# A selective scan with the decays of every third tile made in two column halves

## The chip, the cores and the metric

The kernel runs on one core of a Trainium2 chip. The metric is the device time of one execution in microseconds (us); less is better. The engines of the core are TensorE (PE in the profile, its weight loads PEld), VectorE (DVE), ScalarE (ACT), GpSimd (POOL) and SyncE (SP), which issues the DMAs. Each takes its instructions in the order in which they were written and waits on semaphores for the others.

## The reference

Two layers are computed on `x` of shape 8 x 64 x 64 x 96, in float32. The second, an MLP at doubled resolution with low-pass filters on both sides, fills time between the steps of the first. The first is a two-dimensional selective scan (SS2D); its core, cut to what matters, is this:

```python
# K = 4 directions, D_INNER = 192 channels, D_STATE = 16 states, L = 64*64 steps
def step(h, inp):
    ul, dl, Bl, Cl = inp
    dA = jnp.exp(dl[..., None] * A)                              # the decays
    h = dA * h + (dl * ul)[..., None] * Bl[:, :, None, :]        # the scan
    y = jnp.einsum('bkdn,bkn->bkd', h, Cl)                       # sum over the states
    return (h, y)
...
x = x + L0(group_norm(x))   # projection, 3x3 convolution, scans, layer norm, gate, projection
x = x + L1(group_norm(x))   # upsample, W1, quadratic, W2, low-pass, downsample
```

## The kernel before

An image, a direction and a chunk of `T` = 1024 steps have 192 x 16 state rows. They are cut into `NT` = 24 tiles of 128 partitions (8 channels x 16 states) and 1024 columns (steps). Eight images, four directions and four chunks make 3072 tiles. `t["i"]` is the number of a tile within its chunk, 0 to 23.

What a tile goes through, with the lines of the profile:

- `fetch` (L1063): a DMA brings `dub`, delta times input, spread over the 16 states.
- `product_b` (L1069): GpSimd multiplies it by `br` into `bb`, the scan's additive term.
- `decay` (L1075, L1082): TensorE spreads delta (`dl`) over the 16 states with a selection matrix `sel_b`. Two matmuls of 64 rows, one for each half of the columns, each fill one 2 KB bank of the tile `pd` (128 x 1024 float32 in PSUM, two banks). Float32 matmuls run as two passes, so the profile shows four. Then ScalarE takes the exponential of `pd` in place, scaled by `neg_a`, one number for each partition.
- `scan` (L1089): VectorE runs the recurrence over the 1024 columns. Its result overwrites `pd`, or, where the tile is a "GpSimd tile", goes into `h` in SBUF.
- `product_c` (L1095): the result times `cr` gives `hc`. Every third tile (`by_pool`, where `i % 3 == 2`) has this on GpSimd, from `h`; the others have it on VectorE, from `pd`.
- `hold` (L1108): the last column is copied to `carry` for the next chunk, by ScalarE in a GpSimd tile, by VectorE in the others.
- `sums` (L1127, L1139): TensorE sums `hc` over the states into `py`, for two tiles at a time; `store` copies it out (L1160).

`pd` has two buffers (`psd`, `bufs=2`), so the decay of a tile can begin once the tile two before it has released its buffer. In a GpSimd tile the scan itself releases it; otherwise the product and the copy of the carry do.

The order is written out by hand, in one loop over the tiles. In turn `i` these are issued: `fetch` six tiles ahead, the GpSimd product of the tile before, `product_b` three tiles ahead, `decay` of the next tile, then `scan`, `product_c` and `hold` of this one:

```python
if 0 < i <= n and tiles[i - 1]["by_pool"]:
    product_c(tiles[i - 1])
if i + LEAD < n:
    product_b(tiles[i + LEAD])
if i + 1 < n:
    decay(tiles[i + 1])
if t:
    scan(t)
    if not t["by_pool"]:
        product_c(t)
    hold(t)
```

After that `side.advance` hands out pieces of the other work (projections and the preparation of the next chunk, the convolution, layer norm, the MLP's rows) within a budget for each engine and turn (`CAPS`), `turn_over` (L1101) puts in a filler matmul `idle` where the side work gave TensorE little, and the sums follow. The budgets know neither the scans nor the decays; their costs are in no plan.

So on VectorE a GpSimd tile's scan is followed at once by the next tile's scan, unless side work of VectorE lies between; the other scans are followed by a product and a copy. The framework derives the semaphores from which tiles the instructions touch.

Of the kernel before, what the change touches and what calls it, by code (L numbers as in the profile page):

```python
# [9 lines left out]
AF = mybir.ActivationFunctionType  # L10
# [14 lines left out]
MB = 512  # L25
# [111 lines left out]
def kernel(ctx: ExitStack, tc: tile.TileContext, a: dict, out: bass.AP):  # L137
    nc = tc.nc
# [53 lines left out]
    neg_a = cp.tile([128, K, NT], F32, name="neg_a")  # L192
# [10 lines left out]
    sel_b = cp.tile([128, 8, NS, 8], F32, name="sel_b")  # L203
# [838 lines left out]
    for b in range(images):  # L1042
        for k in (1, 0, 2, 3):
            order = range(NCH) if k < 2 else range(NCH - 1, -1, -1)
            for n, c in enumerate(order):
                got = {}
                for i in range(NT):
                    q, n8 = divmod(i, 8)
                    s, j = n8 % 2, n8 // 2
# [20 lines left out]

    def decay(t):
        pd = t["pd"] = psd.tile([128, T], F32, tag="pd", name="pd")
        for hf in range(2):
            rows = slice(64 * hf, 64 * hf + 64)
            nc.tensor.matmul(  # L1075
                pd[:, MB * hf : MB * hf + MB],
                sel_b[rows, 4 * t["s"] + t["j"]].rearrange("p n c -> p (n c)"),
                t["got"]["dl"][rows, t["q"], :],
                start=True,
                stop=True,  # L1080
            )
        nc.scalar.activation(pd, pd, AF.Exp, scale=neg_a[:, t["k"], t["g"] : t["g"] + 1])  # L1082

    def scan(t):
        step = 1 if t["k"] < 2 else -1
# [86 lines left out]
    with tc.manual_schedule():  # L1172
# [3 lines left out]
        start, rest = front(0)  # L1176
# [8 lines left out]
        n = len(tiles)  # L1185
        for i in range(FETCH):
            fetch(tiles[i])
            if i >= FETCH - LEAD:
                product_b(tiles[i - FETCH + LEAD])
        decay(tiles[0])  # L1190
        begin, *side.later = prepare(0, tiles[NT]["k"], tiles[NT]["i0"], tiles[NT]["got"])
        total = 1
        for i in range(n + 4):
            t = tiles[i] if i < n else None
            at = i % (NT * NCH * K)
            if t and t["i"] == 0:
                b = t["b"]
                if at == 0:
# [9 lines left out]
                    if b + 1 < images:  # L1208
                        start, rest = front(b + 1)
# [31 lines left out]
            if i + 1 < n:  # L1241
                decay(tiles[i + 1])
# [110 lines left out]
```

## Time and profile before

| | |
|---|---|
| time of three runs | 11110.65, 11111.8, 11118.07 us; median 11111.8 |
| profiled execution | span of 11105.8 us from first to last instruction, 6.0 us below the median run; its time outside the span is not in the page |
| granted TensorE clock | 0.982 |
| PE busy | 9967.9 us, of it 3512.7 in the decays' matmuls and 932.0 in the filler |
| DVE busy | 10207.5 us |
| ACT busy | 5910.6 us, of it 3340.7 in the decays' exponentials |
| POOL busy | 10179.6 us |
| scan, 128 x 1024 | 2.34 to 2.35 us (2.28 to 2.29 in a direction's first chunk) |
| product on VectorE, on GpSimd | 1.23 us, 2.36 us |
| exponential, 128 x 1024 | 1.09 us |

A row of the costliest groups reads: line, engine, operation, output and inputs, shapes, count, then busy us and mean ns of one, then idle time of the engine just before, and what ended most of it. A wait is put down to the event that came last by the profile. The slowest core is the only one.

### The profile page before, as it was taken

Reading aid. Unit: us, or ns where it says so; the run is one execution under the profiler, and the core shown is the slowest. Engines: PE = TensorE matmul, PEld = TensorE weight load, DVE = VectorE, ACT = ScalarE, POOL = GpSimd, SP = SyncE. Lnnn points to the kernel's source line nnn. Section 1 sums busy time; section 2 is a strip of 40 time slices with the busy share of each in tenths; the row PEclk is TensorE's granted clock in tenths of the full one; section 3 lists DMA queues with packets and bytes.
Section 4 is the critical chain, followed back from the end, with each engine's and each line's share of the span. In section 5 each row is a group of like instructions: output and inputs, shape, how many; then the busy total and the mean of one; then the engine's idle time right before and its main releaser. Section 6 shows DMA issues by size and latency. Waiting matters only on the chain. (4 is left out here: it accounts for less than half of the span.)

```text
span 11105.8 us, 137238 instructions
## 1 busy us (share of the span) xinstructions
PE 9967.9 (90%) x45020; PEld 3204.6 (29%) x45020; DVE 10207.5 (92%) x7702; ACT 5910.6 (53%) x8218; POOL 10179.6 (92%) x4674
## 2 busy tenths in 40 slices
PE   8898888989889998999889998899988989889988
PEld 2222222322233222332223322233222332223325
DVE  6999999999999999999999999999999999999990
ACT  5455445656455564555545555455554655545543
POOL 5999999999999999999999999999999999999990
PEclk9999999999999999999999999999999999999998
DMA  6888898898988989888988989889898898988981
GB/s 174 215 208 224 209 231 209 217 227 232 233 209 216 225 231 225 212 218 224 240 217 215 224 221 244 209 219 225 217 243 210 217 228 218 247 206 216 227 214 48
DMA packets 1044463, 2401.27 MB, mean 216 GB/s; under 512 B 293820, under 2 KB 314556, under 8 KB 1043752
## 3 DMA queue, kind: packets, MB, share of 16 engines
q1 hardware_dynamic: 1042776, 2391.45, 86.5%
q8 instruction: 361, 5.91, 0.2%
q14 instruction: 350, 2.87, 0.1%
q10 hardware_dynamic: 976, 1.04, 0.0%
HBM read 1929.05 MB, written 328.73 MB: 203 GB/s over the span
## 5 line engine op out<-in xcount | busy, mean ns | idle before, releaser
L1069 POOL TENSOR_TENSOR bb<-dub,br 128x1024 f32<-128x1024 f32 x3072 | 7173.5, 2359 | 208.4 <-DMA dub<-du 149.2
L1082 ACT ACTIVATE pd<-pd,neg_a 128x1024 f32<-128x1024 f32 x3072 | 3340.7, 1088 | 4533.0 <-PE pd L1075 4489.8
L1075 PE MATMUL pd<-dl,sel_b 64*128 64x512 f32 x12288 | 3512.7, 645 | 987.2 <-DVE carry L1108 649.2
L1089 DVE TENSOR_TENSOR_SCAN pd<-pd,carry,bb 128x1024 f32<-128x1024 f32 x1536 | 3610.3, 2350 | 262.2 <-ACT carry L1108 127.9
L1095 POOL TENSOR_TENSOR hc<-h,cr 128x1024 f32<-128x1024 f32 x1024 | 2413.9, 2357 | 352.6 <-DVE h L1089 300.7
L1095 DVE TENSOR_TENSOR hc<-pd,cr 128x1024 f32<-128x1024 f32 x2048 | 2508.4, 1225 | 164.1 <-PE py L1127 20.0
L1075 PEld LDWEIGHTS pd<-dl,sel_b 64*128 64x128 f32 x12288 | 966.7, 186 | 3266.3 <-issue 1511.2
L1089 DVE TENSOR_TENSOR_SCAN h<-pd,carry,bb 128x1024 f32<-128x1024 f32 x768 | 1797.3, 2340 | 5.8 <-ACT pd L1082 5.6
L1127 PE MATMUL py<-hc,sel_r 128*32 128x512 f32 x12288 | 1715.0, 617 | 30.4 <-POOL hc L1095 30.2
L1089 DVE TENSOR_TENSOR_SCAN pd<-pd,bb 128x1024 f32<-128x1024 f32 x512 | 1172.5, 2290 | 98.6 <-ACT carry L1108 75.3
L1101 PE MATMUL idle<-sel_b,ident 128*128 128x512 f32 x1652 | 932.0, 646 | 8.0 <-DVE ty L720 5.9
L562 PE MATMUL pc<-pad,convr 96*128 96x512 f32 (+1 forms) x2304 | 858.3, 616 | 5.7 <-DVE e L585 3.6
L1089 DVE TENSOR_TENSOR_SCAN h<-pd,bb 128x1024 f32<-128x1024 f32 x256 | 583.6, 2280 | 26.0 <-ACT pd L1082 25.2
L1127 PEld LDWEIGHTS py<-hc,sel_r 128*32 128x32 f32 x12288 | 250.3, 109 | 1109.0 <-issue 854.5
L1031 POOL TENSOR_TENSOR u<-dl,u 128x512 f32<-128x512 f32 x384 | 485.0, 1271 | 79.2 <-DVE dl L1028 79.2
L862 PEld LDWEIGHTS p<-w2q,mq 128*100 128x100 f32 x4800 | 452.9, 168 | 274.6 <-issue 214.2
L855 PE MATMUL ph<-xu,w 96*128 96x500 f32 x960 | 504.9, 629 | 11.5 <-ACT mq L856 6.7
L862 PE MATMUL p<-w2q,mq 128*100 128x96 f32 x4800 | 511.5, 258 | 2.3 <-ACT mq L856 2.3
L562 PEld LDWEIGHTS pc<-pad,convr 96*128 96x128 f32 (+1 forms) x2304 | 266.3, 163 | 563.9 <-issue 552.8
L987 PE MATMUL px<-u,xp 64*64 64x512 f32 x1536 | 422.4, 627 | 2.4 <-issue 2.4
L1101 PEld LDWEIGHTS idle<-sel_b,ident 128*128 128x128 f32 x1652 | 249.8, 189 | 596.5 <-issue 522.4
L1012 PE MATMUL pv<-xd,dt_w 64*64 64x512 f32 x1536 | 394.4, 609 | 1.0 <-ACT xd L997 1.0
(153 smaller groups left out, 6707.9 us busy)
## 6 DMA issues: line engine op xcount, KB each, us to landing
dub<-du SPq DMA_DIRECT2D x3072, 512.0 KB
u<-u SPq DMA_DIRECT2D x256, 384.0 KB
du<-u SPq DMA_DIRECT2D x768, 128.0 KB
y<-yq SPq DMA_DIRECT2D x768, 128.0 KB
br<-xd SPq DMA_DIRECT2D x256, 256.0 KB
cr<-xd SPq DMA_DIRECT2D x256, 256.0 KB
yp<-y SPq DMA_DIRECT2D x384, 128.0 KB
yp<-u SPq DMA_DIRECT2D x192, 128.0 KB
```

Source lines behind the costliest of these rows:

```text
L562: nc.tensor.matmul(t[rows].rearrange("p (i j) -> p i j", i=8), weights[:, cs], v["pad"][:, 8 * blk + kw : 8 * blk + kw + 8, kh : kh + H], ...
L855: nc.tensor.matmul(t[:, :px], w1[:, m, :], xu, start=True, stop=True)
L862: nc.tensor.matmul(t[:SIDE, C * i : C * i + C], sq[:, m, row], w2q[:, m, :], start=(m == 0), stop=(m == 2))
L987: nc.tensor.matmul(p[rows], xp[rows, k, q, :], v["u"][rows, q, :], start=(q == 0), stop=(q == 2), skip_group_check=True,)
L1031: nc.gpsimd.tensor_tensor(v["u"][:, q, :], got["dl"][:, q, :], v["u"][:, q, :], ALU.mult)
L1069: nc.gpsimd.tensor_tensor(t["bb"], t["dub"], t["got"]["br"], ALU.mult)
L1075: nc.tensor.matmul(pd[:, MB * hf : MB * hf + MB], sel_b[rows, 4 * t["s"] + t["j"]].rearrange("p n c -> p (n c)"), t["got"]["dl"][rows, t[" ...
L1082: nc.scalar.activation(pd, pd, AF.Exp, scale=neg_a[:, t["k"], t["g"] : t["g"] + 1])
L1089: nc.vector.tensor_tensor_scan(t["h"][:, ::step], pd[:, ::step], t["bb"][:, ::step], 0.0 if t["first"] else held, ALU.mult, ALU.add)
L1095: (nc.gpsimd if t["by_pool"] else nc.vector).tensor_tensor(t["hc"], t["h"], t["got"]["cr"], ALU.mult)
L1101: nc.tensor.matmul(p, ident, sel_b[:, 0:4].rearrange("p j n c -> p (j n c)"), start=True, stop=True)
L1127: nc.tensor.matmul(py[r0 : r0 + 32], sel_r[:, t["j"], :], t["hc"][:, MB * hf : MB * hf + MB], start=(t["j"] == 0), stop=(t["j"] == 3 and t ...
```

## The change

In `decay`, the tiles with `i % 3 == 0`, those that follow a GpSimd tile, are made in two column halves. The halves are cut within each bank: first columns 0 to 255 of both banks, by two matmuls of 256 columns, and their exponential as one instruction over 128 x 2 x 256; then columns 256 to 511 of both banks in the same way. The other tiles are as before. `skip_group_check` is a flag of the build and adds no instruction.

```diff
     def decay(t):
         pd = t["pd"] = psd.tile([128, T], F32, tag="pd", name="pd")
-        for hf in range(2):
-            rows = slice(64 * hf, 64 * hf + 64)
-            nc.tensor.matmul(
-                pd[:, MB * hf : MB * hf + MB],
-                sel_b[rows, 4 * t["s"] + t["j"]].rearrange("p n c -> p (n c)"),
-                t["got"]["dl"][rows, t["q"], :],
-                start=True,
-                stop=True,
-            )
-        nc.scalar.activation(pd, pd, AF.Exp, scale=neg_a[:, t["k"], t["g"] : t["g"] + 1])
+        parts = 2 if t["i"] % 3 == 0 else 1
+        w = MB // parts
+        scale = neg_a[:, t["k"], t["g"] : t["g"] + 1]
+        for c0 in range(0, MB, w):
+            for hf in range(2):
+                rows = slice(64 * hf, 64 * hf + 64)
+                nc.tensor.matmul(
+                    pd[:, MB * hf + c0 : MB * hf + c0 + w],
+                    sel_b[rows, 4 * t["s"] + t["j"]].rearrange("p n c -> p (n c)"),
+                    t["got"]["dl"][rows, t["q"], c0 : c0 + w],
+                    start=True,
+                    stop=True,
+                    skip_group_check=True,
+                )
+            part = pd.rearrange("p (a t) -> p a t", a=2)[:, :, c0 : c0 + w] if parts > 1 else pd
+            nc.scalar.activation(part, part, AF.Exp, scale=scale)
```

## Prediction

> **What bounds the kernel now.** First the page: busy shares, and PE in 40 slices.
>
> ```profile
> PE 9967.9 (90%) x45020; PEld 3204.6 (29%) x45020; DVE 10207.5 (92%) x7702; ACT 5910.6 (53%) x8218; POOL 10179.6 (92%) x4674
> PE   8898888989889998999889998899988989889988
> ```
>
> Three engines stand at 90 to 92%, so no share names the bound; it has to be read from waits. Next, the chain of waits on DVE, which runs all scans (waiting line, releaser, us in total, times, longest):
>
> ```profile
> DVE pd L1089 <- ACT carry L1108: 203.2, 414, 3.6
> DVE pd L1089 <- ACT pd L1082: 113.8, 238, 8.0
> DVE pd L1089 <- POOL bb L1069: 40.2, 38, 2.3
> ```
>
> The scans wait for ScalarE 652 times, 317.0 us in all, and hardly for GpSimd. The label "carry" is the last ACT event before the scan; the timeline shows what was really awaited (start, length, engine, line):
>
> ```profile
> 5014.67 0.15 DVE L1108 COPY carry<-pd 128x1 f32<-128x1 f32 x1
> 5014.74 2.34 DVE L1089 TENSOR_TENSOR_SCAN h<-pd,carry,bb 128x1024 f32<-128x1024 f32 x1
> ...
> 5014.97 1.13 PE L1075 MATMUL pd<-dl,sel_b 64*128 64x512 f32 x4 [1.31 <-DVE carry L1108]
> ...
> 5016.02 0.64 PE L914 MATMUL pn<-ident,x 128*96 128x128 f32 x4
> 5016.13 1.09 ACT L1082 ACTIVATE pd<-pd,neg_a 128x1024 f32<-128x1024 f32 x1 [2.77 <-PE pd L1075]
> ...
> 5017.32 2.36 DVE L1089 TENSOR_TENSOR_SCAN pd<-pd,carry,bb 128x1024 f32<-128x1024 f32 x1 [0.24 <-ACT carry L1108]
> ```
>
> The scan at 5014.74 is a GpSimd tile's (it writes h). Its successor is a tile of the change. The successor's `pd` comes free when DVE has copied the carry (5014.82); four profiled matmuls (two program matmuls, two passes each) end at 5016.10, the exponential at 5017.22, and 0.10 later the scan starts. DVE was done at 5017.08 and idled 0.24 us. After the other tiles DVE has a 1.23 us product and a copy to do, which cover the same chain; after a GpSimd tile it has not. Read tile by tile, in 622 of the 1024 changed tiles the scan starts within 0.15 us of its exponential's end; in the other 402 the median slack is 0.35 us. So DVE paces the kernel, and ahead of every third scan the chain matmul, exponential, scan sets DVE's pace.
>
> Last, one stretch of an image in windows of 100 us (busy us of each engine, instructions):
>
> ```profile
> 3277.00:3377.00 100.00, 95.76 (x541) 40.05 (x541) 96.43 (x74) 60.09 (x86) 97.22 (x44) 1.00 0.92 220
> 3377.00:3477.00 100.00, 97.60 (x540) 38.86 (x538) 96.00 (x59) 61.78 (x82) 97.03 (x45) 1.00 0.87 214
> 3477.00:3577.00 100.00, 96.49 (x543) 38.91 (x541) 96.07 (x76) 59.91 (x86) 98.63 (x46) 1.00 0.88 223
> ...
> 3777.00:3877.00 100.00, 98.95 (x398) 26.66 (x397) 95.31 (x75) 53.56 (x70) 94.98 (x43) 1.00 0.85 214
> 3877.00:3977.00 100.00, 95.78 (x392) 25.23 (x388) 95.44 (x76) 59.30 (x82) 93.30 (x43) 1.00 0.84 213
> ...
> 4077.00:4177.00 100.00, 85.45 (x324) 21.40 (x324) 95.98 (x72) 57.79 (x77) 89.81 (x41) 0.98 0.93 237
> ```
>
> First column: PE. In five of the fourteen windows from 2777 to 4177 PE is 96 to 99% busy: there it bounds beside DVE, with 4.24, 2.40, 3.51, 1.05 and 4.22 us left, 3.08 on average. In the other nine 8.8 to 16.2 us are left.
>
> **What the built order of the change shows.** DVE, GpSimd and the DMA queue keep their instructions and order. PE gets 2048 program matmuls more (4096 profiled), ACT 1024 exponentials. In every split tile the third matmul (second half, first row group) waits for ScalarE's semaphore at the count that the first half's exponential sets. Both halves write both banks of `pd` (columns 0 to 255 of each, then 256 to 511), and the exponential of a half spans both. So the halves do not overlap: matmul, exponential, matmul, exponential run one after the other.
>
> **The chain, step by step.** The costs of a half:
>
> ```profile
> L1082 ACT ACTIVATE pd<-pd,neg_a 128x1024 f32<-128x1024 f32 x3072 | 3340.7, 1088 | 4533.0 <-PE pd L1075 4489.8 <-DVE pd L1089 22.3 <-DVE h L1089 5.8
> L712 ACT ACTIVATE pn<-pn,eps 96x512 f32<-96x512 f32 x64 | 41.8, 653 | 26.0 <-PE pn L710 26.0
> ```
>
> Exponential of 512 columns: 0.65 us, by L712, in place in PSUM with one pointer operand; bounds 0.54 (half of 1.088) and 0.70 (L997, 696 ns). The Trainium skill, "ScalarE: Activation LUTs", What ACT_TABLE_LOAD costs, gives 280 ns plus 0.833 ns an element with one pointer operand: an estimate of 0.71 for a half, 1.13 for the whole that the trace has at 1.09; by it the two halves together grow against the whole by 0.08 more, and the total by some 60 us. Matmuls of a half: 0.64 us, by the four 128-column ones of L914 (512 columns one after another, as here two passes of 256, the row groups side by side); bounds 0.57 (half of 1.13) and 0.70 (0.06 for two exposed weight loads). PE to ACT takes 0.05 us or less here, ACT back to PE 0.05 (shortest pair, L997 to L1012).
>
> Now 1.13 + 0.05 + 1.09 = 2.27. Then 0.64 + 0.05 + 0.65 + 0.05 + 0.64 + 0.05 + 0.65 = 2.73. The chain grows by **0.46 us**; by the bounds by 0.10 to 0.68. In 622 tiles nothing covers it: 622 x 0.46 = 286 us. In the other 402 DVE's own side work covers part; what remains of 0.46 beyond each tile's slack sums to about 45. Together 331 us, over the 10716 us that the scans take 3.09 per 100 us.
>
> PE is held from the first matmul to the last for 0.64 + 0.05 + 0.65 + 0.05 + 0.64 = 2.03 instead of 1.13: **0.90 us** longer. Queued behind the waiting matmul are the sums into `py`, the side work's matmuls (convolutions, projections, MLP), the idle filler and the next decay. With 9.56 changed tiles per 100 us that is 8.60. In nine windows of fourteen PE's own gaps of 8.8 or more hide it; were they gone it would cost what the full windows pay. In the five full windows it does not fit: if the gaps shrink from 3.08 to 1.05, the fullest window's, 2.03 is swallowed and 6.57 is left. That covers the 3.09 of the scan chain there (the two lie side by side).
>
> Sum per 100 us: 5/14 x 6.57 + 9/14 x 3.09 = 2.35 + 1.99 = 4.33; times 107.2 gives **464 us**. The profiled span of 11105.8 becomes 11570. The median run, 11111.8, lies 6.0 above that span; with the same on top, **11576 us**.
>
> What costs nothing: ACT waits some 0.69 us between its halves, 710 us in all, with the carry copy, the copies out of `py` and side activations behind it; ACT sits idle 4533 us before exponentials today, and that is the cover. Gone, it would be 0.69 us in each tile. The next decay after a changed one comes 0.90 later on PE while DVE moves by 0.46; the 0.44 between lies under that tile's median slack of 0.72 (lower quartile 0.43), read tile by tile like those above; the quarter below it is part of what the full windows pay. Weight loads (4096 more) run beside matmuls but for the first, which the 0.64 holds.
>
> The trace of before never shows an exponential beginning before all matmuls of its tile have ended. The Trainium skill, "PSUM — Partial Sum Buffer", PSUM bank collisions raise a hardware error, says that two engines may not touch one bank in the same 32 partitions at once, even at disjoint columns, and that semaphores should guard by bank. By this rule the wait must be there, and the sum is the one above; were only the columns to count, it would be the first rival's.
>
> **Rivals.** *Not slower: the halves overlap.* If the first half's exponential were past when PE reaches the third matmul, ACT would run its first half beside the second matmuls: 0.64 + 0.05 + 0.65 + 0.65 = 1.99, 0.28 less than 2.27. Then waits such as the 0.24 at 5017.32 vanish: 622 x 0.24 = 149 us, 10963. It decides from the point where the third matmul comes less than 0.29 us after the second's end instead of 0.75 (0.64 + 0.29 + 0.64 + 0.05 + 0.65 = 2.27, as today). For it speaks only the change's shape; against it the semaphore count. 3%.
>
> *GpSimd or slack absorbs most.* GpSimd is at 95% in the full windows; if PE's lateness vanishes in its queues and the halves cost 0.60, only the scan chain counts, grown by 0.36: 622 x 0.36 + 23 = 247, to 331 at most: 11359 to 11443. For it: next tiles' slack. Against: scans wait for GpSimd 40 us in all. 22%.
>
> *PE becomes the bound.* If its gaps do not shrink in any stretch, since they are waits for DVE that only move, each tile pays 0.90: 1024 x 0.90 = 922, 12034. For it: PE at 96 to 99% in a third of the time. Against: 8.8 us and more free elsewhere. 8%. *Nothing measurable* (within 0.2%, some 22 us, about what a measurement here tells from no change): 3%.
>
> **Numbers.** The forecast has 64%: 11576, itself 11440 to 11710. The range, 11380 to 11790, reaches down to most of the absorbing case and up by the dearest half: 8.6 kept whole in the full windows (5/14 x 8.6 = 3.07) and the chain grown by 0.64 in the others (622 x 0.64 + 86 = 484 us, 4.52 per 100; 9/14 of it 2.90) give 5.97 per 100 us or 640 us, 11752, and the dearest half, 0.68, some 20 more; the end is set a little above for the PE-bound case. Faster 3%, same 3%, slower 94%.
>
> **What would show it.** Right: 256-column matmuls in two bursts with an exponential of about 0.65 between them; PE waiting about 0.7 us for ACT at the decay line, near 1000 times; scans after GpSimd tiles idle 0.7 us instead of 0.24; the windows full of PE work lengthened most. Wrong: an ACT half that starts before the last matmul of the other has ended (overlap); halves of 0.54; DVE's waits for ACT at 317 us or below; or the full windows growing no more than the light ones, which strikes the PE term.

## The result, and the profile after

The changed kernel takes 11880.73 us (median of 4 runs), the kernel before in the same session 11114.93: a ratio of 1.069 (95% interval 1.0676 to 1.0704), 766 us more. Slower, as forecast, but outside the range and 302 us beyond the 464 of the sum. The profiled execution has a span of 11882.6 us and a mean granted clock of 0.970 (0.982 before).

The page after, busy shares and PE in 40 slices:

```profile
PE 10337.2 (87%) x49116; PEld 3534.4 (30%) x49116; DVE 10260.5 (86%) x7702; ACT 6144.7 (52%) x9242; POOL 10204.4 (86%) x4674
...
PE   8888888988889888898888888888888989889888
```

The shares of PE, DVE, ACT and POOL all fell: none of the four became busier by as much as the span grew. The time went into waits. Line numbers shift from kernel to kernel: the decay's matmuls and exponential, L1075 and L1082 before, are L1079 and L1088 here, the scan, L1089 before, is L1095. The chain of waits, PE's and then DVE's (who waits, for whom, us, times, longest):

```profile
PE pd L1079 <- ACT pd L1088: 852.6, 1024, 6.6
PE pd L1079 <- DVE carry L1114: 394.3, 536, 2.6
PE pd L1079 <- DVE hc L1101: 186.6, 189, 3.3
```

```profile
DVE pd L1095 <- ACT pd L1088: 847.6, 784, 9.1
DVE pd L1095 <- issue: 141.6, 264, 1.5
...
DVE pd L1095 <- POOL bb L1069: 40.7, 53, 1.5
```

The first line is the wait that the built order showed: in all 1024 split tiles PE waits for an exponential, 0.83 us on average. DVE's waits for ScalarE ahead of scans whose result goes to `pd` rose from 317.0 us to 847.6, with a further 141.6 without a named releaser. One split tile and its successor on the timeline:

```profile
549.83 0.15 DVE L1114 COPY carry<-pd 128x1 f32<-128x1 f32 x1
549.90 2.28 DVE L1095 TENSOR_TENSOR_SCAN h<-pd,bb 128x1024 f32<-128x1024 f32 x1
...
550.13 0.70 PE L1079 MATMUL pd<-dl,sel_b 64*128 64x256 f32 x4 [1.47 <-DVE carry L1114]
550.87 0.66 ACT L1088 ACTIVATE pd<-pd,neg_a 128x512 f32<-128x512 f32 x1 [2.26 <-PE pd L1079]
...
551.59 0.70 PE L1079 MATMUL pd<-dl,sel_b 64*128 64x256 f32 x4 [0.75 <-ACT pd L1088]
...
552.22 2.07 PE L1107 MATMUL idle<-sel_b,ident 128*128 128x512 f32 x2
...
552.39 0.66 ACT L1088 ACTIVATE pd<-pd,neg_a 128x512 f32<-128x512 f32 x1 [0.86 <-PE pd L1079]
...
553.14 2.30 DVE L1095 TENSOR_TENSOR_SCAN pd<-pd,bb 128x1024 f32<-128x1024 f32 x1 [0.97 <-ACT pd L1088]
...
554.22 1.74 PE L1133 MATMUL py<-hc,sel_r 128*32 128x512 f32 x8
...
555.89 1.13 PE L1079 MATMUL pd<-dl,sel_b 64*128 64x512 f32 x4
...
557.07 1.09 ACT L1088 ACTIVATE pd<-pd,neg_a 128x1024 f32<-128x1024 f32 x1 [3.42 <-PE pd L1079]
...
557.15 0.15 DVE L1114 COPY carry<-pd 128x1 f32<-128x1 f32 x1
...
558.26 2.30 DVE L1095 TENSOR_TENSOR_SCAN pd<-pd,bb 128x1024 f32<-128x1024 f32 x1 [0.96 <-ACT pd L1088]
```

Three parts of the loss can be seen in it. *The chain:* from 550.13 to 553.05 it runs matmul, exponential, matmul, exponential, 2.92 us (median over the split tiles 2.94, against 2.27 before), and DVE idles 0.97 us. *The hold:* PE leaves the tile at 552.29 instead of 551.26, so filler, sums and the next decay (555.89) come late, and DVE idles 0.96 us once more ahead of the successor's scan at 558.26. *The clock:* the profile has a granted clock of 0.50 from 552.2 to 555.6; the filler takes 2.07 us and the eight matmuls into `py` 1.74, where they took 1.02 and 1.06 at the full clock. So in this example the clock has as much to do with the successor's 0.96 us as the hold has.

Read tile by tile, DVE's idle time ahead of the scans, by the place of the tile (us):

| kernel | tile after a GpSimd tile (split in the change) | the next | GpSimd tile |
|---|---|---|---|
| before | 311 | 36 | 32 |
| after | 828 | 200 | 35 |

517 of the 766 us lie ahead of the split tiles' own scans, 164 ahead of their successors'. (Summed over every gap of the trace, the first column is 9 to 21 us higher in all the kernels below; the differences hardly change.) Of the idle time ahead of the successors 133 us fall on the 132 tiles for which the clock stood at 0.50 somewhere between the split decay and the end of their own. That shows where the low clock is, not what it costs; e13 below measures that.

### The profile page after: what moved, and what is told of

It reads as the page before. It is cut to its first block, busy times and chain, and to the rows that moved or that the text cites. A ratio compares the mean times of both kernels' runs of the same rounds, so it can differ in the third digit from the quotient of the medians.

```text
span 11882.6 us, 147253 instructions
## 1 busy us (share of the span) xinstructions
PE 10337.2 (87%) x49116; PEld 3534.4 (30%) x49116; DVE 10260.5 (86%) x7702; ACT 6144.7 (52%) x9242; POOL 10204.4 (86%) x4674
## 3 DMA queue, kind: packets, MB, share of 16 engines
q10 hardware_dynamic: 976, 1.04, 0.0%
## 5 line engine op out<-in xcount | busy, mean ns | idle before, releaser
L1088 ACT ACTIVATE pd<-pd,neg_a 128x512 f32<-128x512 f32 (+1 forms) x4096 | 3580.9, 874 | 5075.4 <-PE pd L1079 4945.1
L1079 PE MATMUL pd<-dl,sel_b 64*128 64x256 f32 (+1 forms) x16384 | 3834.3, 542 | 1462.7 <-ACT pd L1088 852.6
L1095 DVE TENSOR_TENSOR_SCAN pd<-pd,carry,bb 128x1024 f32<-128x1024 f32 x1536 | 3614.0, 2353 | 757.2 <-ACT pd L1088 613.1
L1079 PEld LDWEIGHTS pd<-dl,sel_b 64*128 64x128 f32 x16384 | 1285.4, 188 | 4173.1 <-issue 1559.2
L1095 DVE TENSOR_TENSOR_SCAN h<-pd,carry,bb 128x1024 f32<-128x1024 f32 x768 | 1798.0, 2341 | 16.4 <-ACT pd L1088 12.5
L1095 DVE TENSOR_TENSOR_SCAN pd<-pd,bb 128x1024 f32<-128x1024 f32 x512 | 1174.6, 2294 | 291.3 <-ACT pd L1088 234.5
L1107 PE MATMUL idle<-sel_b,ident 128*128 128x512 f32 x1652 | 972.4, 672 | 0.4 <-DVE ty L720 0.4
L1095 DVE TENSOR_TENSOR_SCAN h<-pd,bb 128x1024 f32<-128x1024 f32 x256 | 584.1, 2282 | 19.3 <-ACT pd L1088 18.1
```

The lines of the kernel that those rows point to most:

```text
L1079: nc.tensor.matmul(pd[:, MB * hf + c0 : MB * hf + c0 + w], sel_b[rows, 4 * t["s"] + t["j"]].rearrange("p n c -> p (n c)"), t["got"]["dl"][ ...
L1088: nc.scalar.activation(part, part, AF.Exp, scale=scale)
L1095: nc.vector.tensor_tensor_scan(t["h"][:, ::step], pd[:, ::step], t["bb"][:, ::step], 0.0 if t["first"] else held, ALU.mult, ALU.add)
L1107: nc.tensor.matmul(p, ident, sel_b[:, 0:4].rearrange("p j n c -> p (j n c)"), start=True, stop=True)
```

## Experiments

Differences are against the kernel before in the same session (11110 to 11121 us).

**Split without the hold (e1).** The four matmuls first, then both exponentials: all the change's instructions, no matmul waiting for ScalarE.

```diff
-            part = ...
-            nc.scalar.activation(part, part, AF.Exp, scale=scale)
+        for c0 in range(0, MB, w):
+            part = ...
+            nc.scalar.activation(part, part, AF.Exp, scale=scale)
```

> Split as in the change, but all four matmuls of a split tile are issued before its two exponentials: the same number of instructions on every engine, and no matmul waits for an exponential. Theory A (the loss is the chain, longer by 0.67 us in the changed kernel's trace, plus PE held between the halves): the chain becomes about 1.33 + 0.05 + 0.66 + 0.05 + 0.66 = 2.75 us, 0.48 over the 2.27 of before; 622 x 0.48 + 47 = 346 us, PE held only some 0.2 us longer, in all 11400 to 11500. Rival R1 (the split work as such costs it, 4096 more matmuls and 1024 more exponentials, whatever waits for what): 11880 as in the changed kernel. Rival R2 (PE's hold alone costs it, DVE's chain is covered): 0.2 of 1.03 us of hold, some 150 us, 11265.

Measured: 11209.29, ratio 1.0084 (1.0068 to 1.0099), 89 us. So R1 falls: the split work as such does not cost 766 us. The same timeline rows in this kernel:

```profile
5011.24 1.14 PE L1079 MATMUL pd<-dl,sel_b 64*128 64x256 f32 x8 [1.47 <-DVE carry L1115]
...
5012.41 1.36 ACT L1089 ACTIVATE pd<-pd,neg_a 128x512 f32<-128x512 f32 x2 [2.53 <-PE pd L1079]
```

Back to back, eight half-width matmuls take 1.14 us, no longer than four whole ones (1.13); only apart do they cost 2 x 0.70. The two exponentials take 1.36 instead of 1.09. My 1.33 for the eight was wrong, and the chain grew by 0.26 us (median), not 0.48. The slack sum, each tile's growth less its slack, added up as in the prediction, makes 169 us of 0.26; the run pays about half of it.

**The matmuls alone (e2), the exponentials alone (e3).**

```diff
# e2: decay() of the change with one exponential after all four matmuls
-            part = ...; nc.scalar.activation(part, part, AF.Exp, scale=scale)
+        nc.scalar.activation(pd, pd, AF.Exp, scale=scale)
# e3: the kernel before, with
+        for part in (pd[:, :MB], pd[:, MB:]) if t["i"] % 3 == 0 else (pd,):
+            nc.scalar.activation(part, part, AF.Exp, scale=scale)
```

> Only the matmuls of every third tile are split, its exponential is one instruction again, after all four. A: chain 1.33 + 0.05 + 1.09 = 2.47, 0.20 over before: 622 x 0.20 and a little, 127 us, and as much as 40 for PE's 0.2 us: 11240 to 11280. R1: the matmuls' share of the 766 us, some half, 11500. R2: 11265 (does not part from A here).

Measured: 11119.55, ratio 0.9999 (0.9989 to 1.0008). Splitting the matmuls costs nothing where no wait lies between them; A's 127 us rested on the 1.33.

> Matmuls whole as before; in every third tile two exponentials of 512 columns, one for each bank. A: chain 1.13 + 0.05 + 0.66 + 0.06 + 0.66 = 2.56, 0.29 over before, PE not held: 199 us at 0.30, 11300 to 11320. R1: the exponentials' share of 766 us, 11500. R2: PE is not held, 11112 as before.

Measured: 11227.87, ratio 1.0097 (1.0082 to 1.0112), 108 us for a chain longer by 0.26. R2 (the hold is everything) falls, since nothing held PE here. But 0.26 by the slack sum would be some 170 us; the run pays 0.64 of it. Halves by bank did not overlap either: in none of the 1024 tiles does the first bank's exponential start before all four matmuls have ended, and the last passes of the two banks end 0.04 us apart.

**The split elsewhere (e4, e9).** A' in what follows is theory A as revised after e1 to e4: a longer chain costs less than its slack sum, and the hold comes on top, at the next decay behind it.

```diff
-        parts = 2 if t["i"] % 3 == 0 else 1
+        parts = 2 if t["i"] % 3 == 2 else 1     # e4; == 1 in e9
```

> The split as in the change, on the GpSimd tiles themselves (i % 3 == 2) instead of those after them: their chain has a median slack of 1.0 us, so a chain longer by 0.67 shows in few. But PE's hold of 1.03 us ends right ahead of the decay of the tile after, which has no slack in 622 cases. A: by the slack of each tile in the trace of before, 88 us for the chain and 485 for the hold beyond it: 11600 to 11700. Chain alone (no weight for the hold): 11200. R1: 11880.

Measured: 11843.33, ratio 1.0653 (1.0635 to 1.0671), 723 us, almost the change's loss, though the split tiles' own chains are covered. DVE's waits say whose scans are late:

```profile
DVE pd L1095 <- ACT carry L1114: 653.6, 563, 5.4
DVE pd L1095 <- ACT pd L1088: 318.0, 320, 8.0
DVE h L1095 <- ACT pd L1088: 93.7, 176, 6.1
```

The split tiles write `h` and wait 93.7 us. The scans into `pd` wait 971.6: the hold makes the decay of the next tile late, and here that is the one without slack (939 us of idle ahead of those scans, 311 before). The 573 us expected were too few, but the clock stands between: at 0.962 it is lower than the change's 0.970, and 93 of the decays without slack took over 1.3 us instead of 1.13 (22 before). How much of the 150 us beyond the expectation is the clock's, and how much the hold's, this run does not tell.

> The split on the tiles ahead of the GpSimd tiles (i % 3 == 1): their chain has a median slack of 0.72 us, and the decay after it, the GpSimd tile's, one of 1.0 us. A': by the slacks of the trace of before the longer chain (0.67) comes through with 161 us and the hold (1.03) beyond it with 113: 11390, the cheapest of the three places. Rival R1 (the split work as such): 11880 here too, as in both other places.

Measured: 11568.86, ratio 1.0409 (1.0395 to 1.0423), 458 us at a clock of 0.988. The cheapest place, as expected, but dearer than 274: the idle time is 170, 147 and 450 us ahead of split tile, successor and the one after, so tiles up to two decays on are late.

**Chain without hold, hold without chain, both.** e5 makes the exponential in four pieces (chain +0.79 us by its median), e14 in four or three in turn (+0.66 on average); e6 adds a filler matmul behind the decay, e15 does both.

```diff
# e14 (e5: all four cuts whenever i % 3 == 0)
+        cuts = (0, T) if t["i"] % 3 else (0, 256, 512, 768, T) if t["i"] % 6 else (0, 256, 512, T)
+        for c0, c1 in zip(cuts, cuts[1:]):
+            nc.scalar.activation(pd[:, c0:c1], pd[:, c0:c1], AF.Exp, scale=scale)
# e6, and e15 on top of the above
+        if t["i"] % 3 == 0 and side.free:
+            p = side.again(side.free[0], "idle")
+            nc.tensor.matmul(p, ident, sel_b[:, 0:4]..., start=True, stop=True)
```

> Matmuls whole; in every third tile (i % 3 == 0) the exponential is made in four pieces of 256 columns. Each piece beyond the first lengthened the chain by 0.26 us in the run by bank, so the chain grows by about 0.78, more than the changed kernel's 0.67, and PE is held no longer than before. Theory A', revised (a longer chain in a tile without slack costs about 0.64 of what its slack says, as in the run by bank, and PE's hold comes on top, on the next tile's decay): first order 622 x 0.78 + 120 = 605 us, times 0.64 is 390: 11500. Theory C (the chain is all that counts in the changed kernel, the hold nothing): 0.78 / 0.67 x 766 = 890 us, 12000.

Measured: 11624.49, ratio 1.0453 (1.0435 to 1.0470), 504 us: more than the 390 that the share of the run by bank gave, far less than C's 890.

> The decays as before; after the decay of a tile with i % 3 == 0 one more filler matmul (1.02 us of PE, nobody waits for it) wherever a side bank is free, 659 of 1024 times. PE is held as the wait between the halves holds it, the tile's own chain is as before. A': by the gaps and slacks of the trace of before a hold of 1.03 us makes the next tile's scan late by 362 us over 1024 tiles; 659 of them: 230 us, 11350. C (the hold counts for nothing): 11115 to 11140.

Measured: 11444.13, ratio 1.0294 (1.0278 to 1.0309), 324 us, at a clock of 0.985. The profile shows 751.7 us of added filler, and DVE idles 282 us ahead of the successors' scans (36 before). DVE's waits in this kernel (L1092 is the scan, L1082 the exponential):

```profile
DVE pd L1092 <- ACT pd L1082: 343.3, 567, 8.0
DVE pd L1092 <- ACT carry L1111: 232.2, 447, 3.4
```

Together 575.5 us where they were 317.0. A pure hold, with the chain as before and the clock no lower, is worth 3%, and 94 us more than the gaps and slacks of the trace gave.

> Matmuls whole, no hold; the exponential of the tiles with i % 3 == 0 in three pieces or four, in turn, so that the chain grows by 0.26 x 2.5 = 0.65 us, the changed kernel's 0.67. A': between the run by bank (0.26 us, 108 us) and the run in four pieces (0.79 us, 504 us) a straight line gives some 400 us: 11510; what the changed kernel loses beyond that is the hold's. Theory C (the chain is all): 11880.

Measured: 11492.65, ratio 1.0345 (1.0327 to 1.0362), 383 us. C falls: the chain at the changed kernel's length is half of its loss. DVE's largest wait here:

```profile
DVE pd L1092 <- ACT pd L1085: 678.4, 676, 8.5
```

> As the run before, with the extra filler of 1.02 us after the decay in 659 of the 1024 tiles. A': chain and hold together make up the changed kernel's loss; added up from the single runs 400 + 326 = 726, less what the later DVE hides of the hold: 550 to 730, 11670 to 11850. If the two do not add (one hides the other): 11510 to 11560.

Measured: 11658.51, ratio 1.0493 (1.0477 to 1.0508), 549 us, just under the band: the hold adds 166 to the chain, half of the 324 that it costs alone. DVE, late by the chain, hides that part.

The idle time ahead of the scans, columns as above:

| kernel | after a GpSimd tile | the next | GpSimd tile |
|---|---|---|---|
| e3, chain +0.26 | 422 | 14 | 34 |
| e14, chain +0.66 | 742 | 7 | 15 |
| e6, hold | 335 | 282 | 44 |
| e15, both | 798 | 66 | 27 |

With the chain alone the other columns fall: while DVE waits, PE catches up (the next decay begins 0.02 us ahead of the split tile's scan in the median of e14, 0.56 after it before, 1.10 after it in the changed kernel). That is part of why a longer chain alone costs less than the slack sum: in e14 the other two columns give back 46 us. The split tiles' own column grows by 431, against 498 by the sum; those 67 us are not explained.

**The clock (e10 to e13).** e13 puts a short filler into the hold of the changed kernel:

```diff
             nc.scalar.activation(part, part, AF.Exp, scale=scale)
+            if parts > 1 and c0 == 0 and side.free:
+                p = side.again(side.free[0], "idle")
+                nc.tensor.matmul(p[:, :w], ident, sel_b[:, 0:2]..., start=True, stop=True)
```

> The changed kernel with a short filler matmul (256 columns, some 0.55 us of PE) between the halves, where PE only waits, in the 659 split tiles with a free side bank. The order is otherwise that of the change, and the filler fits into the wait of 0.75. A' (PE is held, and that delays the queue; the clock is a small part): 11820 to 11890. Rival K (the hold costs by the clock, which falls because PE idles between the halves): the clock returns to 0.98 and the time falls by 150 us or more, below 11730.

Measured: 11811.97, ratio 1.0628 (1.0613 to 1.0644); 702 us over before, 64 less than the change. The clock:

```profile
core 0: 11800.6 us, clock 0.979
```

Just below what A' expected and far above K's bound: with the clock most of the way back, most of the loss is still there, so the clock is the smaller part. The 64 us are not all of it: PE stands at half clock for 396 us before, 703 in the change and still 508 here.

e10 and e11 leave out the fillers behind the decays of tiles with `i % 3 == 0`, in the changed kernel and in the one before; e12 leaves out, before, those ahead of these decays.

```diff
-            turn_over()
+            if i % 3 != 2:      # e10, e11; != 1 in e12
+                turn_over()
```

> The changed kernel without the filler matmuls of those turns in which the split decay is issued (278 of 826 fillers; each stands on PE between the split decay and the next tile's). A' (PE's hold pushes the next decay): those next decays come up to 1.02 us earlier where PE was behind, the 200 us that DVE idles ahead of the tiles after the split ones shrink to about 120, 11780 to 11830. Rival (the clock: PE idles between the halves, the fillers keep it granted): the clock falls below 0.97 and the time rises, 11900 or more.

Measured: 11845.08, ratio 1.0658 (1.0642 to 1.0673), clock 0.964. It gains 32 us over the change, not the 50 to 100 expected, and the clock falls too: both theories have their effect, and the run does not weigh them.

> The same fillers left out of the kernel before: control for the run above. A': the tiles concerned idle DVE by only 36 us here, so at most some 20 us are gained, 11100; if the clock falls more than it gains, 11120 to 11160.

Measured: 11120.00, ratio 1.0009 (1.0000 to 1.0018): no clear difference.

> The kernel before without the fillers that stand on PE ahead of the decay of the tiles after GpSimd tiles (278 of 826), the decays without slack. A': where PE's backlog makes these decays late, up to 1.02 us is gained; most begin at the release of pd and gain nothing: 11070 to 11110, a version that could beat both. Rival (clock): 11120 or more.

Measured: 11218.58, ratio 1.0093 (1.0079 to 1.0107): slower. The clocks of e12 and the kernel before:

```profile
core 0: 11215.2 us, clock 0.960
```

```profile
core 0: 11105.8 us, clock 0.982
```

Of the 1024 decays that follow a GpSimd tile's, 113 now take over 1.3 us instead of 1.13, 22 before: the rival held. DVE's idle time grew mostly one tile further on, by 71 us ahead of the next tiles' scans and by 23 ahead of these.

**Releasing `pd` earlier (e7; e8 with the split).** The chain could begin 1.4 us sooner if the tile before the GpSimd tile did not keep its `pd` through its product.

```diff
+        t["early"] = t["i"] % 3 == 1            # scan into hc, carry copied ahead of the product
-        t["h"] = sp.tile(...) if t["by_pool"] else pd
+        t["h"] = sp.tile(...) if t["by_pool"] else t["hc"] if t["early"] else pd
```

> No split. The tile before a GpSimd tile scans into its hc tile instead of into pd, its carry is copied ahead of its product, and the product is made in place in SBUF: pd is released 1.4 us earlier, so the decay of the tile after the GpSimd tile can begin before the GpSimd tile's scan. A': the 311 us that DVE idles ahead of those scans shrink to what PE's backlog leaves, some 100: 10900 to 10950. Rival: a product with both inputs in SBUF next to GpSimd is slower than the 1.23 us from PSUM (no row of the traces shows one); at 2.3 it would cost 1.1 us in 1024 tiles, 12100.

Measured: 12197.59, ratio 1.0968 (1.0951 to 1.0984). The waits aimed at did go, from 311 to 71 us, but the rival held. Products and GpSimd's `bb` (line, shapes, busy, mean ns, idle):

```profile
L1099 DVE TENSOR_TENSOR hc<-hc,cr 128x1024 f32<-128x1024 f32 x1024 | 2469.9, 2412 | 35.3
...
L1099 DVE TENSOR_TENSOR hc<-pd,cr 128x1024 f32<-128x1024 f32 x1024 | 1254.3, 1225 | 73.6 <-PE py L1131 3.9 <-issue 0.9
```

```profile
L1069 POOL TENSOR_TENSOR bb<-dub,br 128x1024 f32<-128x1024 f32 x3072 | 7963.8, 2614 | 129.0 <-DVE hc L1092 101.0 <-DMA dub<-du 15.2 <-DVE pd L1092 9.7
```

With both inputs in SBUF the product takes 2.41 us instead of 1.23, and GpSimd's grows from 2.36 to 2.61. The Trainium skill, "SBUF — State Buffer", Who interferes with whom, states it: a VectorE instruction with two SBUF inputs contends with a GpSimd instruction that reads SBUF. The trace agrees: the shortest of these products takes 1.22 us, as from PSUM, the longest 8.3, so it is not the two inputs alone. The 1.19 us in 1024 tiles are 1219 us. Against them stand 240 us of waits saved, less some 160 of new ones: the early scans write into `hc`, whose buffers the sums on PE release (172.5 us of waits for `py`). DVE's idle time fell by 136 us in all, and 1219 - 136 = 1083 is what was lost, to within 10 us.

> The early release together with the change's split. A': the chain's 0.67 us now fits in the released 1.4 us, PE's hold of 1.04 stays and meets the next decay: 200 to 350 us over the early release alone. C: equal to the early release alone.

Measured: 12554.74, ratio 1.1293 (1.1276 to 1.1310), 357 us over e7, just above the 200 to 350 expected. C falls again. DVE's idle time grew by 248 us, about 100 of it ahead of the split tiles' own scans, so their chain is covered mostly and not wholly; 131 are further waits for the sums on PE (303.3 us against 172.5), which the hold makes late. The products with both inputs in SBUF grew from 2.41 to 2.49 us, another 78.

No version beat the kernel before.

## Why the prediction was wrong

**Direction and order of events: right.** The halves do not overlap, PE waits 1024 times, the split tiles' scans are late. "Matmul, exponential, matmul, exponential run one after the other" held in every split tile: no third matmul starts before the first exponential has ended, and the overlapping rival had nothing to stand on. The wait between the halves is what the Trainium skill, "PSUM — Partial Sum Buffer", PSUM bank collisions raise a hardware error, asks for; what an unguarded overlap would do no run here shows. What failed is how the loss was added up: two sizes, two covers that did not cover, and a term left out.

**"The chain grows by 0.46 us": mis-sized, 0.67.** The rows of the changed kernel give the terms:

```profile
L1088 ACT ACTIVATE pd<-pd,neg_a 128x512 f32<-128x512 f32 x2048 | 1354.0, 661 | 2154.0 <-PE pd L1079 2150.0
```

The exponential of a half, 0.65, is 0.66. The matmuls of a half, 0.64, are 0.70, the upper bound; and the second exponential starts 0.11 us after its matmuls, not 0.05 (it waits for PE and for ScalarE's own semaphore). 0.70 + 0.05 + 0.66 + 0.05 + 0.70 + 0.11 + 0.66 = 2.93. I had taken the row of four 128-column matmuls for a pair of row groups in two passes; by this row it was 0.06 too short, and why no run tells. With 0.67 in place of 0.46, and the hold at 1.04, the same sum gives 629 us instead of 464: the sizes are 165 of the 302 us that were missing.

**"In nine windows of fourteen PE's own gaps of 8.8 or more hide it": wrong.** This is the first half of the step that failed: the cover. Matched tile by tile, the same fourteen windows grew by 11.0 us per 100 where PE had been full and by 5.7 where it had not; the forecast was 6.57 and 3.09. The chain alone (e14) makes 4.5 and 3.1 of that, so hold and clock cost 2.6 in windows that I had called covered (e13's fillers take 0.9 of it back, which is the clock's). A gap in a window of 100 us does not help a decay that comes 1 us after the hold. PE's waits before show where the gaps lie:

```profile
PE pd L1075 <- DVE carry L1108: 649.2, 796, 4.7
PE pd L1075 <- DVE hc L1095: 283.0, 273, 3.3
PE pd L1075 <- DVE h L1089: 43.0, 65, 2.3
```

975 of PE's 1123 idle us stand at decays that wait for `pd`; read tile by tile, only 63 lie between a changed tile's decay and the next, where they could have taken up the hold. The pure hold, e6, shows the cost: 2.3 per 100 in the light windows, 5.0 in the full ones. Nor did the gaps foretell which window would pay: the nine light ones grew by anything from -0.5 to 11.1.

**"That covers the 3.09 of the scan chain there (the two lie side by side)": wrong, the other half.** In the full windows the chain alone (e14) costs 4.5 per 100, the chain with 659 fillers as hold (e15) 6.9, the change 11.0. What the change has beyond e14, 6.5 for hold and clock, is near the 6.57 of the forecast; the chain came on top of it and was not covered. Weighted by 5/14 and 9/14 the two failed covers are worth 1.6 and 1.7 per 100 us, the larger sizes within them. That e14's 3.1 in the light windows equals the forecast's 3.09 is luck: the chain was longer than forecast, and paid less than its slack sum.

**The clock: no term at all.** The sum holds PE at the clock of before. It fell from 0.982 to 0.970, and e13 puts at least 64 us on that.

**"The 0.44 between lies under that tile's median slack of 0.72": wrong with it.** A median is no cover. The next tile's scans that start right behind their exponential went from 12% to 31%, and their waits from 36 to 200 us.

**What hid the error.** The slack sum for the chain alone is too high (e14: 383 against some 498 by the sum), in part since PE catches up while DVE waits. In the changed kernel the hold takes that recovery away.

**The 766 us**, as far as settled: 383 by the chain (e14), 64 by the clock (e13). The hold as queue was measured on top of that chain as 166 us with 659 fillers of 1.02 us (e15); in proportion to 1024 tiles that would be 258, which is an estimate. 61 us stay open; parts measured in different kernels need not add exactly. Some of it may be the clock that e13 did not bring back: it took away 195 of the 307 us that the change adds at half clock, in proportion some 100 us for the whole, an estimate. And e14's chain is a little short for the comparison: it grew by 0.66 us on average, the change's by 0.73 (0.67 is the median).

**Of the signs named:** PE's wait near 1000 times, the 0.66 exponential, and the full windows growing most came as said. The scans' median wait is 0.91 us where they wait at all, not 0.7. The absorbing rival, 22%, is out, though a late DVE does hide half of the hold (e15). PE's hold counted in light windows too, as in the third rival, but two of the nine did not grow at all, and it did not add up to 922. ACT's wait between its halves, put at 0.69, is 0.74 by the prediction's own terms; it was 0.89 on average.

## What to carry to other kernels

Before cutting an operation in halves so that two engines overlap, look in the built order for a wait between the halves. If there is one, the chain grows by every fixed cost in it, and the engine that waits in the middle keeps its whole queue for that time. Price such a hold at the next critical instruction behind it, tile by tile, and not from gaps averaged over a window. Take that price as a lower bound: tile by tile the slacks of the trace of before gave 230 us where a pure hold cost 324 (e6), and 274 where the split on the tile ahead cost 458 (e9).

## What the runs showed of the hardware

- Half-width float32 matmuls on two row groups cost nothing extra back to back (eight in 1.14 us, four whole ones in 1.13), but 0.70 us for four when they stand alone.
- Exponentials that follow each other in the same tile cost 0.26 us for each further piece of the same 1024 columns (1.36 us for two pieces, 1.89 for four, 1.09 whole).
- Which fillers are left out matters to the clock: without those ahead of the critical decays, a third of all, it fell from 0.982 to 0.960 and the kernel lost 107 us; without those behind them it stood at 0.978 and the kernel lost nothing clear.
- A VectorE product is 1.23 us with one input in PSUM and 2.41 us on average with both in SBUF beside a busy GpSimd (1.22 at the shortest); GpSimd's own grew from 2.36 to 2.61.
